# Preparing the later layers' weights in nine steps among a convolution's groups

## The chip, the cores and the metric

The kernel runs on one core of one Trainium2 chip. The metric is the device time of one execution in microseconds (us). Before the change the median of three timed runs is 3836.9 us; the three lie between 3829.45 and 3837.47 us. One further execution was profiled: it took 3831.74 us, and its span on the profile (first instruction to last) is 3829.9 us, so 1.84 us lie around the span.

## The reference, cut to what matters

Four layers follow one another on `x` of shape (4, 96, 64, 64), float32. Layer 0 is a pair of scan blocks with a fused normalisation; layer 1 is a depthwise 7x7 convolution and a two-layer perceptron; layer 2 is attention without softmax and a quantised perceptron; layer 3 is a Fourier mixer and another quantised perceptron. The change touches layer 1's convolution and the parameters of everything after it:

```python
# layer 1: the convolution, then the perceptron
h = jax.lax.conv_general_dilated(x, conv_w, window_strides=(1, 1), padding=((3, 3), (3, 3)),
        dimension_numbers=('NCHW', 'OIHW', 'NCHW'), feature_group_count=dim)
h = h + conv_b[None, :, None, None]
h = jnp.transpose(h, (0, 2, 3, 1))
h = (h - mu) * jax.lax.rsqrt(var + LN_EPS) * ln_g + ln_b
h = jax.nn.gelu(jnp.einsum('bhwc,cf->bhwf', h, w1) + b1, approximate=False)
h = jnp.einsum('bhwf,fc->bhwc', h, w2) + b2
h = jnp.transpose(h, (0, 3, 1, 2)) * layer_scale[None]
return h + x
# layer 3's mixer: a normalisation with given mean and variance on each side of it
def _bn(v, gamma, beta, mean, var):
    return (v - mean) * (gamma / jnp.sqrt(var + EPS)) + beta
h = jnp.einsum('bnc,hc->bnh', x, w1)
h = jax.nn.relu(_bn(h, bn1_gamma, bn1_beta, bn1_mean, bn1_var))
...
o = jnp.einsum('bnh,ch->bnc', y, w2)
return _bn(o, bn2_gamma, bn2_beta, bn2_mean, bn2_var)
```

The kernel folds these scales and shifts into the weights once: `ln_g` into `w1`, `ln_b` into `b1`, `layer_scale` into `w2` and `b2`, `bn1` into layer 3's `w1` (with a 97th row for the shift), `bn2` into its `w2`; and it rounds the weights of the two quantised perceptrons to an 8-bit type.

## The kernel before, in words

The program runs layer 0, then layer 1, layer 2, the Fourier mixer and the last perceptron, each with its own tile pools. Layer 1 (`layer1`, L909) has two parts. The first holds a manual schedule for TensorE (PE), VectorE (DVE), ScalarE (ACT) and GpSimd (POOL): on those four engines the instructions stand in the order in which the Python code issues them. The queue of SyncE (SP), which issues every DMA, is not in that list; a scheduler orders it, and it may put a DMA ahead of the place where the code asks for it.

The first part of layer 1 loads layer 0's output in 16 chunks and turns it so that a partition is a pixel position of a pair of image rows (L948 to L953). Then comes the convolution, a loop of 24 groups of four channels (L973). For each group, SP loads a banded matrix `band` of 128 x 2048 float32, 1024 KB (L957), into one of three buffers. PE makes 16 products of 128 x 128 from it (L983 three times and L986 once for each channel), and the result is evicted with the bias from PSUM by ACT for even groups (L993) and by DVE for odd ones (L991), four instructions each. POOL copies `x2` for the products of L986 two groups at a time (L964, L965). The PSUM tile of a group has four buffers (`cv`); a band's buffer is free again when its group's products are done, so the band of group g + 3 can be asked for when group g ends.

Ahead of group 8 stands one call, `consts2` (L975 calls L821), which prepares all later layers' weights. On PE it issues three products for `c_b1` (L836) and two for `a_w2` (L899). On ACT it issues two square roots (L878 for the first norm, L120 for the second). On DVE it issues everything else, in this order: the layer 1 weights (L839 to L846), the two perceptrons' roundings (L860 to L870, once for "f2" and once for "f3"), the first norm (L879 to L884), the second norm (L121 to L890), the scaled identity `bn2_d` (L895) and the copies of `a_w2` out of PSUM (L900). It asks for 17 loads. Three matter below: `wkv` and `a_w1` have 97 partitions, and so has `bn1_rows` (L876), where a row of 4 x 192 numbers is read 97 times, once for each partition:

```python
rows = wk.tile([C + 1, 4, NF], F32, name="bn1_rows")
nc.sync.dma_start(rows, ins["bn1_rows"].partition_broadcast(C + 1))
```

The raw weights of "f2" and "f3" share one buffer for each kind (tags `raww1` and `raww2`), so the second load waits until the first has been rounded.

Of the kernel before, what the change touches and what calls it, by code (L numbers as in the profile page):

```python
# [9 lines left out]
F32 = mybir.dt.float32  # L10
# [3 lines left out]
AF = mybir.ActivationFunctionType  # L14
# [4 lines left out]
B, C, HW, L = 4, 96, 64, 4096  # L19
# [6 lines left out]
HID = 384  # L26
N1, N2, NF = 128, 32, 192
# [75 lines left out]
class Net:  # L103
# [715 lines left out]


    def consts2(self, wk, small):  # L821
        tc, nc, ins = self.tc, self.nc, self.ins
        pool = self.pool2

        def load(name, shape, dtype=F32):
            t = pool.tile(shape, dtype, name=name)
            nc.sync.dma_start(t, ins[name])
            return t


        self.c_w1 = load("c_w1", [C, HID])
        self.c_w2 = load("c_w2", [128, 3, C])
        self.c_b1 = pool.tile([128, 3], F32, name="c_b1s")
        ps = small(128, 4)
        for m in range(3):
            nc.tensor.matmul(  # L836
                ps[:, m : m + 1], self.c_w1[:, m * 128 : (m + 1) * 128], self.v("c_ln_b"), start=True, stop=True
            )
        nc.vector.tensor_add(self.c_b1, self.v128("c_b1", 0, 3), ps[:, :3])  # L839
        nc.vector.tensor_scalar_mul(self.c_w1, self.c_w1, self.v("c_ln_g"))  # L840
        ls = wk.tile([128, C], F32, name="ls_row")
        nc.sync.dma_start(ls, ins["ls_row"].partition_broadcast(128))
        for m in range(3):
            nc.vector.tensor_mul(self.c_w2[:, m, :], self.c_w2[:, m, :], ls)
        self.c_b2 = pool.tile([C, 1], F32, name="c_b2s")
        nc.vector.tensor_mul(self.c_b2, self.v("c_b2"), self.v("c_ls"))  # L846


        self.wkv = load("wkv", [C + 1, 2 * C])
        self.wqt = load("wqt", [C, C + 1])  # L850
        self.wff = load("wff", [C, C])
        self.mask = load("mask", [C, C])


        self.ffn = {}
        for k in ("f2", "f3"):
            a = wk.tile([C, HID], F32, name="w1raw", tag="raww1")
            nc.sync.dma_start(a, ins[f"{k}_w1"])
            w1 = pool.tile([C, HID], F8, name=f"{k}w1q")
            nc.vector.tensor_copy(w1, a, saturate=False)  # L860
            a = wk.tile([128, 3, C], F32, name="w2raw", tag="raww2")
            nc.sync.dma_start(a, ins[f"{k}_w2"])
            w2 = pool.tile([128, 3, C], F8, name=f"{k}w2q")
            nc.vector.tensor_copy(w2, a, saturate=False)
            b1 = pool.tile([128, 3], F32, name=f"{k}b1q")
            b2 = pool.tile([C, 1], F32, name=f"{k}b2q")
            for b, src in ((b1, self.v128(f"{k}_b1", 0, 3)), (b2, self.v(f"{k}_b2"))):
                q = wk.tile(list(b.shape), F8, name="bq", tag=f"bq{b.shape[0]}{k}")
                nc.vector.tensor_copy(q, src, saturate=False)
                nc.vector.tensor_copy(b, q)  # L870
            self.ffn[k] = (w1, w2, b1, b2)


        self.a_w1 = load("a_w1", [C + 1, NF])
        rows = wk.tile([C + 1, 4, NF], F32, name="bn1_rows")
        nc.sync.dma_start(rows, ins["bn1_rows"].partition_broadcast(C + 1))  # L876
        s1 = wk.tile([C + 1, NF], F32, name="bn1_s")
        nc.scalar.activation(s1, rows[:, 3, :], AF.Sqrt, bias=self.eps[: C + 1])  # L878
        nc.vector.reciprocal(s1, s1)  # L879
        nc.vector.tensor_mul(s1, s1, rows[:, 0, :])  # L880
        nc.vector.tensor_mul(self.a_w1[:C], self.a_w1[:C], s1[:C])
        shift = wk.tile([C + 1, NF], F32, name="bn1_b")
        nc.vector.tensor_mul(shift, s1, rows[:, 2, :])
        nc.vector.tensor_sub(self.a_w1[C:], rows[C:, 1, :], shift[C:])  # L884
        r = self.rsqrt(pool, self.v("v2"), "bn2_r")
        self.s2 = pool.tile([C, 1], F32, name="bn2_s")
        nc.vector.tensor_mul(self.s2, r, self.v("g2"))
        self.b2 = pool.tile([C, 1], F32, name="bn2_b")
        nc.vector.tensor_mul(self.b2, self.s2, self.v("m2"))
        nc.vector.tensor_sub(self.b2, self.v("be2"), self.b2)  # L890

        raw = wk.tile([C, NF], F32, name="a_w2raw")
        nc.sync.dma_start(raw, ins["a_w2"])
        gain = wk.tile([C, C], F32, name="bn2_d")
        nc.vector.tensor_scalar_mul(gain, self.ident[:C, :C], self.s2)  # L895
        self.a_w2 = pool.tile([C, 2, C], F32, name="a_w2s")
        for half in range(2):
            ps = small(C, C)
            nc.tensor.matmul(ps, raw[:, half * C : (half + 1) * C], gain, start=True, stop=True)  # L899
            nc.vector.tensor_copy(self.a_w2[:, half], ps)  # L900
        self.dft1 = load("dft1", [N1, 2 * 65])
        self.twid = load("twid", [128, 2, 2 * 65])
        self.dft2 = load("dft2", [128, 3 * 128])
        self.dft64 = load("dft64", [128, 2, 128])

    def layer1(self, scratch, t):  # L909
        tc, nc, ins = self.tc, self.nc, self.ins  # L910
# [3 lines left out]
        with ExitStack() as ctx:  # L914
# [4 lines left out]
            with (  # L919
# [35 lines left out]
                def load(g):  # L955
                    w = wk.tile([128, GC, 4, 128], F32, name="band", tag="band", bufs=3)
                    nc.sync.dma_start(w, ins["band"][g])  # L957
                    return w

                def outer(g):  # L960

                    x2 = wk.tile([128, 2 * GC, B, NR], F32, name="x2", tag="x2", bufs=3)
                    at = slice(g * 2 * GC, (g + 1) * 2 * GC)
                    nc.gpsimd.tensor_copy(x2[:64], xt[:64, at, :, 4:])  # L964
                    nc.gpsimd.tensor_copy(x2[64:], xt[64:, at, :, :NR])  # L965
                    return x2

                def small(rows, cols):
                    ps = psum.tile([128, 4, 128], F32, name="w_ps", tag="xt", bufs=4)
                    return ps.rearrange("p a c -> p (a c)")[:rows, :cols]  # L970

                x2 = [outer(0)]
                for g in range(C // GC):  # L973
                    if g == 8:
                        self.consts2(wk, small)  # L975
                    if g % 2 == 0 and g + 2 < C // GC:
                        x2.append(outer(g // 2 + 1))
                    w = load(g)
                    ps = psum.tile([128, GC, B, NR], F32, name="cv_ps", tag="cv", bufs=4)
                    for d in range(GC):  # L980
                        c = g * GC + d
                        for k, j in enumerate((1, 0, 2)):
                            nc.tensor.matmul(  # L983
                                ps[:, d], w[:, d, j], xt[:, c, :, 1 + j : 1 + j + NR], start=k == 0, stop=False
                            )
                        nc.tensor.matmul(ps[:, d], w[:, d, 3], x2[g // 2][:, g % 2 * GC + d], start=False, stop=True)  # L986
                    for d in range(GC):
                        c = g * GC + d
                        dst = xt[:, c, :, 2 : 2 + NR]
                        if g % 2:  # L990
                            nc.vector.tensor_scalar_add(dst, ps[:, d], cb[:, c : c + 1])  # L991
                        else:
                            nc.scalar.activation(dst, ps[:, d], AF.Identity, bias=cb[:, c : c + 1])  # L993

            wk = ctx.enter_context(tc.tile_pool(name="l1w", bufs=1))
            psum = ctx.enter_context(tc.tile_pool(name="l1p", bufs=1, space=PSUM))
            mv, rs, xc, g = {}, {}, {}, {}
# [684 lines left out]
```

## Time and profile before

| what | before |
|---|---|
| median of three timed runs | 3836.9 us |
| their range | 3829.45 to 3837.47 us |
| the profiled execution's own time | 3831.74 us |
| its span | 3829.9 us |
| busy share of the span: PE, DVE, ACT, POOL | 84%, 78%, 71%, 67% |
| first product of the convolution (PE, L983) | at 2593.17 us |
| first eviction of group 0 (ACT, L993) | at 2601.18 us |
| first eviction of group 23 (DVE, L991) | at 2710.17 us |

All times on the trace count from the start of the span. A row of the timeline gives start, duration, engine, line, operation, output and inputs, sizes, a count, and in brackets how long the engine sat idle before it and what ended that. A matrix product in float32 appears as two instructions on PE, so the 16 products of a group are 32 rows in count. "SPq" rows are the DMA issues of SyncE: their duration is that of the issue, not of the transfer.

### The profile page before, as it was taken

Reading aid. Unit: us, or ns where it says so; the run is one execution under the profiler, and the core shown is the slowest. Engines: PE = TensorE matmul, PEld = TensorE weight load, DVE = VectorE, ACT = ScalarE, POOL = GpSimd, SP = SyncE. Lnnn points to the kernel's source line nnn. Section 1 sums busy time; section 2 is a strip of 40 time slices with the busy share of each in tenths; the row PEclk is TensorE's granted clock in tenths of the full one; section 3 lists DMA queues with packets and bytes.
Section 4 is the critical chain, followed back from the end, with each engine's and each line's share of the span. In section 5 each row is a group of like instructions: output and inputs, shape, how many; then the busy total and the mean of one; then the engine's idle time right before and its main releaser. Section 6 shows DMA issues by size and latency. Waiting matters only on the chain. (4 is left out here: it accounts for less than half of the span.)

```text
span 3829.9 us, 46555 instructions
## 1 busy us (share of the span) xinstructions
PE 3229.4 (84%) x15326; PEld 1475.1 (39%) x15326; DVE 2988.8 (78%) x2644; ACT 2719.1 (71%) x5456; POOL 2569.1 (67%) x922
## 2 busy tenths in 40 slices
PE   7888788888888888888888888657799998999988
PEld 3333233333323332333333333226544534766643
DVE  5999999999999999999999999962573384444649
ACT  6788888877887888788877787641355686666557
POOL 1988888888988888888888888832001064444427
PEclk8899998989998899889988898757899999999999
DMA  7566665666566656665665566556200000011101
GB/s 189 145 157 155 169 157 142 167 153 158 139 165 158 154 142 165 158 152 144 160 163 149 147 160 159 132 143 209 71 1 0 1 1 6 18 37 33 39 9 58
DMA packets 171642, 446.61 MB, mean 117 GB/s; under 512 B 48756, under 2 KB 50750, under 8 KB 168064
## 3 DMA queue, kind: packets, MB, share of 16 engines
q1 hardware_dynamic: 171400, 443.64, 45.2%
q8 instruction: 121, 1.98, 0.2%
q14 instruction: 121, 0.99, 0.1%
HBM read 369.97 MB, written 73.50 MB: 116 GB/s over the span
## 5 line engine op out<-in xcount | busy, mean ns | idle before, releaser
L648 POOL TENSOR_TENSOR hs<-hs,crep 128x2048 f32<-128x2048 f32 x384 | 1599.1, 4184 | 212.8 <-DVE hs L643 115.6
L610 ACT ACTIVATE da<-ddb,nega 128x1024 f32<-128x1024 f32 x576 | 657.8, 1147 | 192.3 <-DVE hs L643 187.4
L643 DVE TENSOR_TENSOR_SCAN hs<-da,state,rep 128x1024 f32<-128x1024 f32 x288 | 667.5, 2337 | 56.6 <-PE rep L594 40.5
L665 PE MATMUL y<-hs,sel_r 128*32 128x512 f32 x3072 | 455.4, 677 | 77.9 <-POOL hs L648 77.9
L621 POOL TENSOR_TENSOR up<-udb,brep 128x1024 f32<-128x1024 f32 x192 | 452.3, 2363 | 70.1 <-DMA udb<-ud 60.4
L594 PE MATMUL rep<-ident,uta 128*128 128x128 f32 x1536 | 242.3, 309 | 163.3 <-DVE hs L643 163.2
L507 ACT ACTIVATE uta<-delta,bt 128x192 f32<-128x192 f32 x1024 | 379.1, 442 | 1.1
L643 DVE TENSOR_TENSOR_SCAN hs<-dap,state,up 128x1024 f32<-128x1024 f32 x144 | 336.7, 2338 | 44.8 <-ACT dap L610 44.8
L643 DVE TENSOR_TENSOR_SCAN hs<-da,state,u 128x1024 f32<-128x1024 f32 x144 | 338.1, 2348 | 15.5 <-DVE u L636 0.5
L287 PE MATMUL ps<-n,w_x 97*64 97x512 f32 x1536 | 347.4, 600 | 1.5 <-ACT n L401 1.5
L594 PEld LDWEIGHTS rep<-ident,uta 128*128 128x128 f32 x1536 | 195.7, 158 | 268.5 <-DVE hs L643 148.8
L610 ACT ACTIVATE dap<-ddb,nega 128x1024 f32<-128x1024 f32 x192 | 213.9, 1114 | 101.3 <-DVE hs L643 100.7
L599 PE MATMUL rep<-dbl,sel_b 32*128 32x512 f32 x768 | 247.4, 723 | 27.8 <-DVE hs L643 27.0
L636 DVE TENSOR_TENSOR u<-udb,rep 128x1024 f32<-128x1024 f32 x192 | 235.7, 1227 | 39.6 <-DMA udb<-ud 13.7
L1240 POOL CAST hq<-y 128x1536 fp8e5<-128x1536 f16 x64 | 94.0, 1469 | 217.8 <-issue 122.6
L287 PE MATMUL ps<-dbl,dtw 103*64 103x512 f32 x384 | 174.4, 960 | 74.5 <-ACT dbl L441 74.5
L636 DVE TENSOR_TENSOR rep<-udb,rep 128x1024 f32<-128x1024 f32 x192 | 231.9, 1208 | 0.0
L643 DVE TENSOR_TENSOR_SCAN hs<-da,rep 128x1024 f32<-128x1024 f32 x96 | 216.8, 2277 | 15.8 <-PE rep L594 10.6
L665 PEld LDWEIGHTS y<-hs,sel_r 128*32 128x32 f32 x3072 | 68.2, 116 | 383.0 <-POOL hs L648 194.8
L287 PEld LDWEIGHTS ps<-n,w_x 97*64 97x64 f32 x1536 | 110.1, 137 | 232.8 <-issue 206.2
L479 POOL TENSOR_TENSOR delta<-delta,xc 128x1536 f32<-128x1536 f32 x31 | 106.6, 3438 | 94.4 <-DMA dd<-delta 87.7
L1379 POOL TENSOR_TENSOR av<-av,ec 128x780 f32<-128x780 f32 x32 | 58.8, 1838 | 133.2 <-ACT av L1376 133.2
(276 smaller groups left out, 6228.6 us busy)
## 6 DMA issues: line engine op xcount, KB each, us to landing
ddb<-dd SPq DMA_DIRECT2D x768, 128.0 KB
udb<-ud SPq DMA_DIRECT2D x768, 128.0 KB
crep<-cd SPq DMA_DIRECT2D x512, 128.0 KB
dd<-delta SPq DMA_DIRECT2D x64, 384.0 KB
band<-in_band SPq DMA_DIRECT2D x24, 1024.0 KB
ud<-delta SPq DMA_DIRECT2D x62, 384.0 KB
brep<-cd SPq DMA_DIRECT2D x128, 128.0 KB
x<-in_x SPq DMA_DIRECT2D x32, 384.0 KB
```

The source lines that it names most:

```text
L287: nc.tensor.matmul(ps[rows], w[:, 64 * p : 64 * p + 64], rhs[:, at.start + shift : at.stop + shift], start=k == 0, stop=k == len(ws) - 1, ...
L479: (nc.gpsimd if k else nc.vector).tensor_mul(m["du"], m["delta"], m["xc"])
L507: nc.scalar.mul(m["uta"][:, q, :, 32 * s4 : 32 * s4 + 32].rearrange("t (p j) d -> t p j d", p=3), m["udt"][:, :, q].rearrange("t p (j d) - ...
L594: nc.tensor.transpose(x[:, q * 128 : q * 128 + 128], made[k]["uta"][:, q, 2 * h + j], self.ident)
L599: nc.tensor.matmul(x[:, at], sel_b[rows, g], made[k]["dbl"][rows, at], start=True, stop=True)
L610: nc.scalar.activation(da, made[k]["dd", h, j], AF.Exp, scale=nega[:, col : col + 1])
L621: nc.gpsimd.tensor_mul(up, made[k]["ud", p][:, j], made[k]["brep", GP])
L636: nc.vector.tensor_mul(u, made[k]["ud", h][:, j], x)
L643: nc.vector.tensor_tensor_scan(hs[:, 1:], made[k].pop(("da", t)), u, st, ALU.mult, ALU.add)
L648: nc.gpsimd.tensor_mul(hs[:, :, :T], hs[:, :, 1:], twice(made[k]["crep", g]))
L665: nc.tensor.matmul(made[k]["y", p][row : row + 32], sel_r, made[k]["hs", p, g][:, j, at], start=False, stop=True, skip_group_check=True,)
L1240: nc.gpsimd.tensor_copy(q, y2, saturate=False)
```

## The change

`consts2` becomes a generator. Its body is cut into nine steps by `yield`; the loop over the groups runs one step ahead of each of the groups 4, 5, 6, 7, 14, 15, 16, 17 and 20, instead of all of it ahead of group 8. The first four steps only ask for loads; the raw weights of "f2" and "f3" get buffers of their own. The next five compute. The four vectors of the first norm are loaded as one row on one partition, the arithmetic on them is done on that one partition, and a product with a column of ones spreads scale and shift over 97 partitions. The rest of the arithmetic is the same.

```diff
-        def load(name, shape, dtype=F32):
-            t = pool.tile(shape, dtype, name=name)
+        def load(name, shape, dtype=F32, into=pool, key=None):
+            t = into.tile(shape, dtype, name=key or name)
             nc.sync.dma_start(t, ins[name])
             return t
         self.c_w1 = load("c_w1", [C, HID])
         self.c_w2 = load("c_w2", [128, 3, C])
+        ls = wk.tile([128, C], F32, name="ls_row")
+        nc.sync.dma_start(ls, ins["ls_row"].partition_broadcast(128))
+        self.wkv = load("wkv", [C + 1, 2 * C])
+        self.wqt = load("wqt", [C, C + 1])
+        yield
+        self.wff = load("wff", [C, C])
+        self.mask = load("mask", [C, C])
+        raw = {k: load(f"{k}_w1", [C, HID], into=wk, key=f"{k}w1raw") for k in ("f2", "f3")}
+        raw |= {k + "2": load(f"{k}_w2", [128, 3, C], into=wk, key=f"{k}w2raw") for k in ("f2", "f3")}
+        yield
+        self.a_w1 = load("a_w1", [C + 1, NF])
+        rows = wk.tile([1, 4, NF], F32, name="bn1_rows")
+        nc.sync.dma_start(rows, ins["bn1_rows"])
+        araw = load("a_w2", [C, NF], into=wk, key="a_w2raw")
+        self.dft1 = load("dft1", [N1, 2 * 65])
+        yield
+        self.twid = load("twid", [128, 2, 2 * 65])
+        self.dft2 = load("dft2", [128, 3 * 128])
+        self.dft64 = load("dft64", [128, 2, 128])
+        yield
...
+        yield
         self.ffn = {}
         for k in ("f2", "f3"):
-            a = wk.tile([C, HID], F32, name="w1raw", tag="raww1")
-            nc.sync.dma_start(a, ins[f"{k}_w1"])
             w1 = pool.tile([C, HID], F8, name=f"{k}w1q")
-            nc.vector.tensor_copy(w1, a, saturate=False)
-            a = wk.tile([128, 3, C], F32, name="w2raw", tag="raww2")
-            nc.sync.dma_start(a, ins[f"{k}_w2"])
+            nc.vector.tensor_copy(w1, raw[k], saturate=False)
             w2 = pool.tile([128, 3, C], F8, name=f"{k}w2q")
-            nc.vector.tensor_copy(w2, a, saturate=False)
+            nc.vector.tensor_copy(w2, raw[k + "2"], saturate=False)
...
             self.ffn[k] = (w1, w2, b1, b2)
-        self.a_w1 = load("a_w1", [C + 1, NF])
-        rows = wk.tile([C + 1, 4, NF], F32, name="bn1_rows")
-        nc.sync.dma_start(rows, ins["bn1_rows"].partition_broadcast(C + 1))
-        s1 = wk.tile([C + 1, NF], F32, name="bn1_s")
-        nc.scalar.activation(s1, rows[:, 3, :], AF.Sqrt, bias=self.eps[: C + 1])
-        nc.vector.reciprocal(s1, s1)
-        nc.vector.tensor_mul(s1, s1, rows[:, 0, :])
-        nc.vector.tensor_mul(self.a_w1[:C], self.a_w1[:C], s1[:C])
-        shift = wk.tile([C + 1, NF], F32, name="bn1_b")
-        nc.vector.tensor_mul(shift, s1, rows[:, 2, :])
-        nc.vector.tensor_sub(self.a_w1[C:], rows[C:, 1, :], shift[C:])
+            yield
+        s1 = wk.tile([1, 2, NF], F32, name="bn1_s")
+        one = wk.tile([1, C + 1], F32, name="bn1_one")
+        nc.vector.memset(one, 1.0)
+        nc.scalar.activation(s1[:, 0], rows[:, 3, :], AF.Sqrt, bias=self.eps[:1])
+        nc.vector.reciprocal(s1[:, 0], s1[:, 0])
+        nc.vector.tensor_mul(s1[:, 0], s1[:, 0], rows[:, 0, :])
+        nc.vector.tensor_mul(s1[:, 1], s1[:, 0], rows[:, 2, :])
+        nc.vector.tensor_sub(s1[:, 1], rows[:, 1, :], s1[:, 1])
...
+        yield
+        ps = small(C + 1, 2 * NF)
+        nc.tensor.matmul(ps, one, s1.rearrange("p k f -> p (k f)"), start=True, stop=True)
+        nc.vector.tensor_mul(self.a_w1[:C], self.a_w1[:C], ps[:C, :NF])
+        nc.vector.tensor_copy(self.a_w1[C:], ps[C:, NF:])
...
+                later = self.consts2(wk, small)
                 x2 = [outer(0)]
                 for g in range(C // GC):
-                    if g == 8:
-                        self.consts2(wk, small)
+                    if g in (4, 5, 6, 7, 14, 15, 16, 17, 20):
+                        next(later)
```

More of the change, by code (lines that the diff above doesn't have):

```diff
@@ L840, in consts2 @@
         nc.vector.tensor_scalar_mul(self.c_w1, self.c_w1, self.v("c_ln_g"))
-        ls = wk.tile([128, C], F32, name="ls_row")
-        nc.sync.dma_start(ls, ins["ls_row"].partition_broadcast(128))
         for m in range(3):
@@ L846, in consts2 @@
         nc.vector.tensor_mul(self.c_b2, self.v("c_b2"), self.v("c_ls"))
[L849 to L852, printed above, removed]
+        yield
         self.ffn = {}
         for k in ("f2", "f3"):
-            a = wk.tile([C, HID], F32, name="w1raw", tag="raww1")
-            nc.sync.dma_start(a, ins[f"{k}_w1"])
             w1 = pool.tile([C, HID], F8, name=f"{k}w1q")
-            nc.vector.tensor_copy(w1, a, saturate=False)
-            a = wk.tile([128, 3, C], F32, name="w2raw", tag="raww2")
-            nc.sync.dma_start(a, ins[f"{k}_w2"])
+            nc.vector.tensor_copy(w1, raw[k], saturate=False)
             w2 = pool.tile([128, 3, C], F8, name=f"{k}w2q")
-            nc.vector.tensor_copy(w2, a, saturate=False)
+            nc.vector.tensor_copy(w2, raw[k + "2"], saturate=False)
             b1 = pool.tile([128, 3], F32, name=f"{k}b1q")
@@ L890, in consts2 @@
         nc.vector.tensor_sub(self.b2, self.v("be2"), self.b2)
-        raw = wk.tile([C, NF], F32, name="a_w2raw")
-        nc.sync.dma_start(raw, ins["a_w2"])
         gain = wk.tile([C, C], F32, name="bn2_d")
         nc.vector.tensor_scalar_mul(gain, self.ident[:C, :C], self.s2)
+        yield
[3 more added lines that the diff above has]
+        nc.vector.tensor_copy(self.a_w1[C:], ps[C:, NF:])
         self.a_w2 = pool.tile([C, 2, C], F32, name="a_w2s")
@@ L898, in consts2 @@
             ps = small(C, C)
-            nc.tensor.matmul(ps, raw[:, half * C : (half + 1) * C], gain, start=True, stop=True)
+            nc.tensor.matmul(ps, araw[:, half * C : (half + 1) * C], gain, start=True, stop=True)
             nc.vector.tensor_copy(self.a_w2[:, half], ps)
[L901 to L904, printed above, removed]
+        yield
     def layer1(self, scratch, t):
```

## The prediction

> **What bounds the kernel now.** The layers run one after the other, so I looked for the stage that the change touches. The page's 40 slices show a dip in PE's busy share (6, 5) and clock (8, 7, 5, 7) around slice 27; the page's chain of waits covers only 14% of the span and does not reach back to it. I then cut layer 1 with the view by windows (window, length, busy us of PE and PEld, DVE, ACT, POOL, granted PE clock, DMA share, GB/s):
>
> ```profile
> 2590.00:2626.00 36.00, 33.25 (x259) 32.53 (x260) 5.55 (x15) 5.38 (x17) 12.45 (x12) 0.85 0.62 213
> 2626.00:2650.00 24.00, 1.72 (x16) 1.67 (x15) 8.38 (x32) 0.64 (x2) 2.07 (x2) 0.61 0.51 167
> 2650.00:2713.00 63.00, 60.05 (x516) 59.86 (x514) 11.00 (x42) 9.16 (x32) 10.38 (x10) 0.96 0.63 218
> ```
>
> PE is full before and after, and works 1.72 us of the 24 between. The convolution is bound by PE, with one hole in it. The timelines of PE, ACT and DVE show what holds it open:
>
> ```profile
> 2622.98 0.91 PE L983 MATMUL cv_ps<-xt,band 128*128 128x128 f32 x6 [0.51 <-DMA band<-in_band]
> ...
> 2626.63 0.73 PE L836 MATMUL w_ps<-vec,c_w 96*128 96x1 f32 x6
> 2649.63 0.93 PE L899 MATMUL w_ps<-bn_d,a_w2raw 96*96 96x96 f32 x4 [22.28 <-DVE bn_d L895]
> ...
> 2622.57 1.14 ACT L993 ACTIVATE xt<-cv_ps,cb 128x128 f32<-128x128 f32 x4 [6.01 <-PE cv_ps L986]
> 2637.37 0.46 ACT L878 ACTIVATE bn_s<-bn_rows,eps 97x192 f32<-97x192 f32 x1 [13.66 <-DMA bn_rows<-in_bn_rows]
> ...
> 2656.51 1.15 ACT L993 ACTIVATE xt<-cv_ps,cb 128x128 f32<-128x128 f32 x4 [18.50 <-PE cv_ps L986]
> ...
> 2626.90 1.13 DVE L991 TENSOR_SCALAR xt<-cv_ps,cb 128x128 f32<-128x128 f32 x4 [6.77 <-PE cv_ps L986]
> ...
> 2644.69 0.35 DVE L860 CAST f3w1q<-w1raw 96x384 fp8e5<-96x384 f32 x1 [13.86 <-DMA w1raw<-in_f_w]
> ```
>
> PE's two `a_w2` products (L899) stand ahead of group 8 and wait 22.28 us for `bn_d`. That is last in DVE's queue, which waits 13.86 us for the raw "f3" weights. SP's own rows say why they are late:
>
> ```profile
> 2615.72 0.30 SPq L876 DMA_DIRECT2D bn_rows<-in_bn_rows  x1
> 2616.06 6.70 SPq L893 DMA_DIRECT2D a_w2raw<-in_a_w  x1
> ...
> 2637.41 0.33 SPq L858 DMA_DIRECT2D w1raw<-in_f_w  x1
> ```
>
> The "f3" load is issued only at 2637.41, when `bn1_rows` has landed, 21.6 us after its issue.
>
> **What the Trainium skill says.** (1) "DMA: Bandwidth & Descriptors", section "Why a DMA increments its semaphore by 16 and not by 1": a load is split over k engines, k the largest number up to 16 that divides the slowest dimension; 96 or 128 partitions give 16. By that rule 97, a prime, gives 1: `bn1_rows`, `a_w1` and `wkv` each go through one engine. The trace agrees in effect: 291 KB took 21.6 us, and the DMA share fell to 0.19 between 2620 and 2625. (2) "TensorE: Matmul & The Clock Gate", Part 1: PE idle for some 3.4 us drops to half clock and needs as long again to return. The trace agrees: after the hole the clock is 0.50 until 2655, and a conv product's instruction takes up to 552 ns there against 273. (3) "Perfetto Trace Analysis", "Per-instruction lifecycle": a DMA's reported duration leaves out the data's movement. Here 0.30 us of issue stand for a 21.6 us load, so I take landing times from who waited.
>
> **The change, part by part.**
>
> *The hole.* Evictions give the cadence: ACT's at 2608.26, 2615.41 and 2622.57 (timeline) are two groups apart, so a group takes 3.58 us. From DVE's for group 7 (2626.90) to ACT's for group 8 (2656.51) it is 29.61: 26.03 too long. That contains 22.28 of waiting, 0.73 for L836, some 0.7 for L899 and about 2.3 of half clock. All goes from this place: **-26.03**.
>
> *The band's wait.* From 2622.57 to 2626.90 is 4.33: group 7 lost 0.75 to its band. It is counted anew below: **-0.75**.
>
> *PE's work that stays.* The three `c_b1` products (0.73) move ahead of group 14, the two `a_w2` products ahead of group 20. At full clock a 128-column product costs 3.58/16 = 0.22 us, so two of 96 columns cost some 0.4 with their start. New is the spreading product, 384 columns: 3 x 0.22 = 0.67. Together **+1.8**.
>
> *DVE, ACT and their waits.* In the order of the built kernel, steps 14 and 15 both stand between DVE's evictions of groups 13 and 15, and steps 16 and 17 between those of 15 and 17. From the DVE rows: 2.1 us for step 14, 1.3 each for 15 and 16, 3.4 for 17. The one-partition form doesn't shorten it: the subtraction on one partition took 0.35 us for 192 columns, like the products on 97. So 3.4 and 4.7 us go into gaps of 6.03: hidden. New wait: DVE's reciprocal waits for ACT's square root, behind ACT's eviction of group 16. If E is the end of group 16 on PE, the root is ready at E + 1.14 + 0.46, the chain of 3.4 ends near E + 5.0, and queued behind it is DVE's eviction of group 17, due at E + 3.6: 1.4 us late. PSUM has four buffers, so PE needs that one at about E + 14: nothing. PE's wait ahead of group 20 is due at E + 10.7, 5.7 us after `bn_d`: nothing. Without that cover each us there would cost one. ACT's two roots (0.74) lie in its 6.01 of idle. POOL's queue is unchanged.
>
> *The loads.* There are 17 as before; SP issues each in 0.3 to 0.4 us, which PE does not see. `bn1_rows` shrinks from 298 kB on one engine to 3 kB. But the other 97-row load, `a_w1` (74.5 kB), now stands before band 6 instead of before band 7, and 590 kB of raw weights stand before band 5. A band is asked for when a buffer frees and is needed 2 x 3.58 = 7.15 us later. I follow the one busy engine, taking it to work in order. Its rate: `bn1_rows` came 14.4 us after band 7 (2622.95 to 2637.37), so 298/14.4 = 20.7 kB/us for short rows. By the "f3" weights' arrival, 7.3 us later, it had moved its sixteenths of two bands and five small loads, 178 kB: 24.3 kB/us. A band's sixteenth (65.5 kB) costs 2.7 us, `a_w1` 3.6. Before: band 6 asked at 2611.8, done 2614.5, `a_w1` 2618.1, band 7 2620.8; PE began at 2622.98, so 2.2 us lie around. After: band 4 asked at 2604.6, done 2607.3; raw weights 1.8, to 2609.1; band 5 to 2611.8; `a_w1` to 2615.4; three small loads to 2616.0; band 6 to 2618.7, usable 2620.9, needed 2618.9: **+2.0**. Then 1.4 for the Fourier tables, band 7 to 2622.8, usable 2625.0, needed 2624.5 (already shifted): **+0.5**. Band 8 is in time. Bounds: 0 if an engine moves the 27 GiB/s that page (1) gives under "Specifications" (an estimate: `a_w1` then takes 2.6 and a band 2.3, and band 6 is usable near 2617.9, in time); 10 if SP is held at two places as at `a_w2raw` (6.70 us), less the cover of some 2 each. Below nothing is excluded: waiting for data cannot gain.
>
> *Sum:* -26.03 - 0.75 + 1.8 + 2.5 = **-22.5**. Against the profiled run, 3831.7 - 22.5 = 3809.2. The median of the timed runs, 3836.9, lies 5.2 above it; the four times known (3829.5, 3831.7, 3836.9, 3837.5) have their middle at 3834.3, and I take that as the base: 3834.3 - 22.5 = **3811.8** is the forecast. What is late next is PE itself: groups at 3.58 to the end; the perceptron follows unchanged.
>
> **The rivals.**
>
> *A, as above,* 3804 to 3818. For it: bands came at PE's pace from 2656 to 2700 with SP waiting on PE each time.
>
> *B, the loads take the hole's place.* Too much before bands 5 to 8 makes PE wait about 2 us at five groups, or 10 at one with a fall of the clock (2.3). Saving 12: 3822. For it: SP was held 6.70 us once, and 5.97 at `wqt` behind `wkv`'s 97 rows. Against: DMA moved 294 to 339 GB/s between 2605 and 2615 without delaying a product.
>
> *C, the steps don't hide.* The chain is late by more than its 5.7 us and PE waits at group 20 as it did from 2644.69 (4.9, and 2.3 of clock). Saving 15: 3819. Against: the gaps above.
>
> *D, slower.* With PE unbroken from 2593 to 2920 its granted clock falls in layer 1's perceptron. PE is busy 224 of the 247 us from 2713. A clock of 0.91 there costs 22 us, the whole gain; 0.87 costs 33, so 3845. It decides from 0.91 down. Against: from 2760 to 3180 the clock is 1.00 with PE nearly full.
>
> **How the numbers follow.** A 0.80, B 0.13, C 0.04, D 0.03. 0.2% is 7.7 us, about what a measurement of this kernel tells from no change. A and C are faster; I give 0.03 of B to "same": faster 0.94, same 0.03, slower 0.03. Range: from the lowest run with no band wait (3829.5 - 25.0 = 3804.5, rounded down to 3803) to B (3822, rounded up to 3823).
>
> **What would show it.** Right: PE's groups 3.58 apart from group 1 to 23 except at groups 6, 7, 14 and 20; the first eviction of group 23 some 86.5 us after that of group 0, instead of 108.99; clock 1.00 from 2605 to the stage's end; no product waiting for `bn_d`. Wrong: waits for `band` of over 5 us, SP rows of several us near `a_w1`, PE idle before L902 or L908, or a lower clock after the convolution.

## The result and the profile after

The changed kernel takes 3807.45 us (median of four runs, 3803.28 to 3811.07), the kernel before 3834.56 us beside it (four runs, 3829.45 to 3837.47). The ratio is 0.9933, 95% interval 0.9921 to 0.9946: a gain of 27.1 us, by the interval 20.7 to 30.3. The profiled execution took 3803.84 us, its span is 3801.7 us.

First the stage that the prediction was about: the view by windows, cut as before at PE's start, at the old hole's place and at the stage's end.

```profile
2583.00:2619.00 36.00, 31.21 (x244) 30.43 (x245) 5.85 (x15) 5.38 (x17) 12.46 (x12) 0.87 0.77 262
2619.00:2643.00 24.00, 23.76 (x213) 23.60 (x213) 3.38 (x12) 3.43 (x12) 6.23 (x6) 1.00 0.81 288
2643.00:2682.00 39.00, 38.15 (x336) 37.27 (x334) 16.57 (x55) 6.22 (x22) 6.41 (x6) 1.00 0.65 227
```

Where PE worked 1.72 of 24 us it now works 23.76, at full clock. DVE's preparation is in the third window (16.57 us busy), beside PE's 38.15 of 39. PE's own timeline shows the waits for bands that are left, and the moved products (two more waits of 0.1 us, at groups 5 and 7, are too short to be marked):

```profile
2613.94 0.91 PE L987 MATMUL cv_ps<-xt,band 128*128 128x128 f32 x6 [2.24 <-DMA band<-in_band]
2632.41 0.91 PE L987 MATMUL cv_ps<-xt,band 128*128 128x128 f32 x6 [0.24 <-DMA band<-in_band]
2643.21 0.73 PE L857 MATMUL w_ps<-vec,c_w 96*128 96x1 f32 x6
2665.43 0.88 PE L902 MATMUL w_ps<-bn_s,bn_one 1*97 1x384 f32 x2
2666.24 0.58 PE L908 MATMUL w_ps<-bn_d,a_w2raw 96*96 96x96 f32 x4
```

No bracket stands behind L902 or L908: PE did not wait for the norms. It waited at group 6 (2.24 us) and a little at group 11 (0.24) for a band. SP's rows around that place:

```profile
2600.90 0.33 SPq L960 DMA_DIRECT2D band<-in_band  x1
2601.27 0.29 SPq L828 DMA_DIRECT2D a_w<-in_a_w  x1
2601.61 2.98 SPq L845 DMA_DIRECT2D bn_rows<-in_bn_rows  x1
...
2605.52 0.37 SPq L960 DMA_DIRECT2D band<-in_band  x1
```

SP is held for 2.98 us at the tiny `bn_rows`, right behind the 97-partition `a_w1` (`a_w` in the rows), and so asks for band 6 about 1 us late: at 2605.52, 0.97 us after the eviction of group 3 began, where bands 3 to 5 were asked for shortly before such an eviction began. PE gets it at 2613.94. SP's own waits tell when `a_w1` landed:

```profile
SPq L960 <- DMA a_w<-in_a_w: 2.7, 1, 2.7
```

The request for band 7 waits 2.7 us for that landing and goes out at 2610.89; 3.05 us later PE has band 6.

The measure used below is the **stage**: from the first eviction of group 0 to the first of group 23. It was 108.99 us (2601.18 to 2710.17) and is 87.37 (2593.89 to 2681.26): 21.62 less. The spans differ by 28.2. The rest lies elsewhere: the stage starts 7.29 earlier, and what follows it takes 0.71 longer (1120.44 against 1119.73).

### The profile page after: what moved, and what is told of

Its sections match the earlier page's. It is cut to its first block, busy times and chain, and to the rows that moved or that the text cites. A ratio compares the mean times of both kernels' runs of the same rounds, so it can differ in the third digit from the quotient of the medians.

```text
span 3801.7 us, 46563 instructions
## 1 busy us (share of the span) xinstructions
PE 3222.8 (85%) x15328; PEld 1469.6 (39%) x15328; DVE 2992.1 (79%) x2646; ACT 2720.4 (72%) x5456; POOL 2569.4 (68%) x922
```

## The experiments

Each kernel is one edit of the kernel before or of the changed one. Stages are read from each one's profiled execution, one for each row. Ratios are to the kernel before on the same chip: its median was 3832.23 us beside the split rows, the one row, the old rows and the split `a_w1`, and 3832.61 beside the four others that are not the two kernels above.

| kernel | stage, us | gained | median, us | ratio, 95% interval |
|---|---|---|---|---|
| before | 108.99 | | | |
| changed | 87.37 | 21.6 | 3807.45 | 0.9933 (0.9921 to 0.9946) |
| before, rows split 96 + 1 | 98.17 | 10.8 | 3816.33 | 0.9964 (0.9950 to 0.9977) |
| before, one row | 99.27 | 9.7 | 3823.57 | 0.9975 (0.9967 to 0.9983) |
| before, own raw buffers | 100.39 | 8.6 | 3826.14 | 0.9984 (0.9977 to 0.9991) |
| changed, old rows | 100.85 | 8.1 | 3824.99 | 0.9983 (0.9976 to 0.9991) |
| changed, computing at group 8 | 98.00 | 11.0 | 3824.72 | 0.9979 (0.9971 to 0.9986) |
| changed, `a_w1` split | 85.79 | 23.2 | 3810.46 | 0.9953 (0.9938 to 0.9968) |
| changed, loads spread evenly | 84.28 | 24.7 | 3808.64 | 0.9940 (0.9926 to 0.9953) |
| changed, once more | 88.22 | 20.8 | 3812.29 | 0.9947 (0.9934 to 0.9960) |

In every row the gain of the stage lies within the interval of the median. The medians alone stray from the stages by up to 5 us (the split rows gain 15.9 by the median, computing at group 8 gains 7.9), so what follows rests on the stages and on the waits within them.

**The rows in two DMAs.** Is it the bytes of `bn1_rows`, or that 97 partitions go through one DMA engine? The bytes stay:

```diff
-        nc.sync.dma_start(rows, ins["bn1_rows"].partition_broadcast(C + 1))
+        nc.sync.dma_start(rows[:C], ins["bn1_rows"].partition_broadcast(C))
+        nc.sync.dma_start(rows[C:], ins["bn1_rows"])
```

> The kernel before, with one edit: bn1_rows is read for 96 partitions in one DMA and for the 97th in a second; same bytes, same place, same arithmetic. Measured on the convolution's stage, from the first eviction of group 0 to the first of group 23 (before 108.99 us, after 87.37). Theory (the hole is held open because a 97-partition load runs through one DMA engine): the rows land within some 4 us, the raw f3 weights are asked for as soon as f2 is rounded (near 2630) and come some 4 us later, PE goes on near 2638 instead of 2649.6: stage 97 to 99 us, some 11 us less in time. Rival (the bytes of the broadcast, or the work in one place whatever the loads): stage stays within 3 us of 109.

Measured: 98.17, within the range of the theory. Of ACT's, DVE's and PE's timelines, the rows that answer to those shown of before:

```profile
2620.69 0.45 ACT L879 ACTIVATE bn_s<-bn_rows,eps 97x192 f32<-97x192 f32 x1 [1.24 <-DMA bn_rows<-in_bn_rows]
...
2629.32 0.36 DVE L860 CAST f3w1q<-w1raw 96x384 fp8e5<-96x384 f32 x1 [1.62 <-DMA w1raw<-in_f_w]
...
2634.22 0.93 PE L900 MATMUL w_ps<-bn_d,a_w2raw 96*96 96x96 f32 x4 [9.99 <-issue]
```

ACT has the rows 9.22 us after their issue at 2611.47, not the 4 us expected, but far from the 21.65 of before. DVE waits 1.62 us for the "f3" weights where it waited 13.86, and PE sits idle 9.99 us where it sat 22.28. The same 291 KB in 96 + 1 partitions shorten the hole by 12.3 us: bytes, place and arithmetic are as before, so it was the 97 partitions in one load (that such a load keeps a single engine busy is shown further down, with the old rows). SP's own waits in the kernel before show how the rows had held up the "f3" load:

```profile
SPq L858 <- DMA bn_rows<-in_bn_rows: 7.3, 1, 7.3
```

The "f2" weights had been rounded by 2630.3, and SP waited on for the rows to land. Of the 12.3 us, 7.3 are this wait; the other 5 are the "f3" load itself, in use 7.28 us after its issue before and 2.33 us here. A part of it comes back: PE now waits 1.63 us for band 7 (0.51 before), though the rows are asked for 0.4 us after that band.

**One row, work still in one place.**

> The kernel before with the changed kernel's one-row form of the first norm (one row, arithmetic on one partition, spreading product), all still ahead of group 8 and the raw weights still sharing buffers. Theory: as with the split rows, stage 97 to 100 us, the product adding 0.7 and some waits; so the row alone is worth about half of the gain of 21.6, and the spreading of the work the other half. Rival (the place of the work is all): stage near 109. Second rival (the row is all): stage near 88.

The edit is the changed kernel's one-row norm put into the old `consts2`. Measured: 99.27, within the range of the theory and far from both rivals. From PE's timeline:

```profile
2639.01 1.56 PE L886 MATMUL w_ps<-bn_s,bn_one 1*97 1x384 f32 x2 [8.79 <-DVE bn_s L884]
2642.38 0.93 PE L903 MATMUL w_ps<-bn_d,a_w2raw 96*96 96x96 f32 x4 [1.81 <-issue]
```

The row removes the late load; what is left, 8.79 and 1.81 us, is DVE's chain, for which PE's products stand and wait. (In the 8.79 are 1.53 us in which DVE waits for the "f3" weights, whose buffers are still shared.) The spreading product is at half clock there, 1.56 us against 0.88 in the changed kernel.

**The steps without the row.**

> The changed kernel with its nine steps, but the first norm in the old form (97-partition broadcast load in the third step, arithmetic on 97 partitions, no spreading product). Theory: the 298 kB on one engine now stand ahead of band 6 and PE waits there for 16 us instead of 2.2, with a fall of the clock: stage 101 to 105 us, so the steps without the row are worth only a third of the gain. Rival (the steps alone do it): stage 86 to 89 us.

The edit puts the 97-partition broadcast and the old arithmetic back into steps three and eight. Measured: 100.85, just under the range of the theory. First PE's timeline, then the view by windows over the wait:

```profile
2630.63 1.62 PE L983 MATMUL cv_ps<-xt,band 128*128 128x128 f32 x6 [15.05 <-DMA band<-in_band]
```

```profile
2610.00:2615.00 5.00, 5.00 (x47) 5.00 (x47) 0.00 (x0) 1.14 (x4) 0.68 (x1) 1.00 0.16 54
2615.00:2620.00 5.00, 0.58 (x6) 0.39 (x4) 1.12 (x4) 0.00 (x0) 2.07 (x2) 0.82 0.75 252
2620.00:2625.00 5.00, 0.00 (x0) 0.00 (x0) 0.00 (x0) 0.00 (x0) 0.00 (x0) 0.50 0.75 251
```

The hole has only moved, from `bn_d` to a band: 15.05 us at group 6. Ahead of it the DMA share is 0.16 at 54 GB/s. SP is held for 5.84 us at `a_w2raw`, behind the broadcast, and asks for band 6 only at 2614.88, so little new comes in. What is under way meanwhile goes through one engine of the sixteen, as a window of one microsecond shows:

```profile
2611.00:2612.00 1.00, 1.00 (x11) 1.00 (x11) 0.00 (x0) 0.00 (x0) 0.00 (x0) 1.00 0.07 23
```

A share of 0.07 is close to one sixteenth, 0.0625. The late request is not what keeps PE waiting: by SP's waits the broadcast lands at 2627.66 (the request for band 8 waits 6.0 us for it), and PE has band 6 2.97 us after that. From the landing of `a_w1` to band 6 it is 3.05 us in the changed kernel, 3.04 with the computing at group 8, 2.97 in the changed kernel's second execution. Band 6 comes last on the engine of the odd load. Spreading the work over the groups does not spread a load that sits on one engine.

**`a_w1` in two DMAs.** What keeps band 6 waiting in the changed kernel?

```diff
-        self.a_w1 = load("a_w1", [C + 1, NF])
+        self.a_w1 = pool.tile([C + 1, NF], F32, name="a_w1")
+        nc.sync.dma_start(self.a_w1[:C], ins["a_w1"][:C])
+        nc.sync.dma_start(self.a_w1[C:], ins["a_w1"][C:])
```

> The changed kernel with a_w1 loaded as 96 partitions and a 97th in two DMAs. Theory (band 6 is late because a_w1 keeps one DMA engine for 3.6 us): the wait of 2.24 us at group 6 goes, stage 84.5 to 85.5 us. Rival (the sixteen engines together are full with 590 kB of raw weights and the bands, the DMA share is 1.0 there): the wait stays near 2, stage 87.

Measured: 85.79, between the two. The wait at group 6 is gone, but two others appear. PE's timeline, then the windows ahead of them:

```profile
2621.27 0.91 PE L989 MATMUL cv_ps<-xt,band 128*128 128x128 f32 x6 [0.16 <-DMA band<-in_band]
2629.62 0.91 PE L989 MATMUL cv_ps<-xt,band 128*128 128x128 f32 x6 [0.95 <-DMA band<-in_band]
```

```profile
2616.00:2621.00 5.00, 5.00 (x46) 4.92 (x45) 1.12 (x4) 0.00 (x0) 2.07 (x2) 1.00 1.05 356
2621.00:2626.00 5.00, 4.84 (x44) 4.76 (x43) 0.80 (x4) 1.14 (x4) 0.78 (x1) 1.00 1.02 386
```

With the load spread all sixteen engines are full (share 1.05 and 1.02, 356 and 386 GB/s; in the changed kernel it is as high there, 1.08 from 2602 to 2605), and a band still comes 0.95 us late; SP, which waits 2.3 us for band 5 to land ahead of a Fourier table, had also asked for it about 1 us late, at 2622.06. So both explanations hold for a part. Beside the kernel in which no band is late (84.28, below) the stage has 1.5 us here, 3.1 in the changed kernel and 3.9 in its second execution: the one engine is half of the lateness or more, the crowding of the loads the rest.

**Computing in one place, loads early.**

```diff
-                    if g in (4, 5, 6, 7, 14, 15, 16, 17, 20):
+                    for _ in range({4: 1, 5: 1, 6: 1, 7: 1, 8: 5}.get(g, 0)):
                         next(later)
```

> The changed kernel with its four loading steps as they are, but its five computing steps all ahead of group 8. Theory (two causes: late loads, and a chain of DVE work that PE must sit out where its own products stand right behind it): the loads are early here, so what is left is DVE's chain, 1.1 for the eviction of group 7 and 8.1 of preparation, less 0.7 of PE's own products, then half a clock (2.3): stage 97 to 100 us, near the split rows. Rival (once the loads are early the place of the computing is free): stage 86 to 89.

Measured: 98.00, within the range of the theory. From PE's timeline:

```profile
2644.24 1.56 PE L902 MATMUL w_ps<-bn_s,bn_one 1*97 1x384 f32 x2 [7.08 <-DVE bn_r L121]
```

With every parameter in time (DVE waits for none) PE still idles 7.08 us ahead of group 8, and then runs at half clock. From group 7's eviction to group 8's it is 16.21 us instead of 3.56. Late bands cost 3.2 us at groups 5 to 7, as in the changed kernel, so what differs is the placing of the computing: it is worth 10.6 of the 21.6.

**Own buffers for the raw weights.**

```diff
-            a = wk.tile([C, HID], F32, name="w1raw", tag="raww1")
+            a = wk.tile([C, HID], F32, name="w1raw", tag=f"raww1{k}")
```

and the same for `w2raw`.

> The kernel before, with one edit: the raw weights of f2 and f3 have buffers of their own, so the f3 loads need not wait for f2's rounding; bn1_rows stays a 97-partition broadcast. Theory: the f3 weights are early, but the broadcast lands near 2638.7 on the scale of the trace before, and DVE's chain for the norms (3.7 us) starts only then: PE goes on near 2643 instead of 2649.6, stage 100 to 104 us, so own buffers alone are worth a quarter to a third of the gain. Rival (the shared buffers were the cause): stage 92 to 96.

Measured: 100.39, within the range of the theory. From ACT's timeline:

```profile
2635.24 0.45 ACT L878 ACTIVATE bn_s<-bn_rows,eps 97x192 f32<-97x192 f32 x1 [14.00 <-DMA bn_rows<-in_bn_rows]
```

The "f3" weights are no longer waited for, and the next one in the row, the broadcast itself, holds ACT for 14.00 us and through it DVE and PE (15.42 us idle). One thing came free: the scheduler moved `a_w1` behind band 7 here, and PE's wait for band 7 (0.51) vanished. That is a second sign of what `a_w1` costs a band behind it.

**Loads spread evenly.** The steps of loading become ten, ahead of the groups 4 to 13, with a few small loads each, and `a_w1` is split; the computing stays. Of the edit, the loop:

```diff
-                    if g in (4, 5, 6, 7, 14, 15, 16, 17, 20):
+                    if g in (4, 5, 6, 7, 8, 9, 10, 11, 12, 13, 14, 15, 16, 17, 20):
```

> The changed kernel with its loads spread over the groups 4 to 13, one or two small ones ahead of each band and at most 180 KB, and a_w1 in 96 partitions and one; computing as it is. Theory: no band is late any more; the stage is 23 x 3.58 and PE's own 2.0, 84.0 to 84.8 us, 3 us less than the changed kernel, which the time itself (runs lie 8 us apart) can hardly show. Rival (bands are late for another reason, the sixteen engines being near their limit all the time): waits of 1 us or more stay somewhere, stage over 85.5.

Measured: 84.28, within the range of the theory. The view of PE's waits from the first product to the stage's end has one row:

```profile
PE cv_ps L1000 <- POOL x L978: 0.6, 1, 0.6
```

It is the wait of the first group for POOL. No band is late, and PE's own added work, 1.94 us, is all that is above 23 groups of 3.58. The median is 3808.64 beside 3812.29 for the changed kernel in the same session: that points the way of the stage's 3.9, but runs of each of these two kernels lie up to 11 us apart and the intervals overlap, so the time alone doesn't show it.

**The changed kernel once more.**

> The changed kernel again, unchanged. Its profiled run gained 28.1 us against the profiled run of before, of which the stage gave 21.6 and the time ahead of it 7.3. Theory (what lies ahead of the stage differs by some us from run to run, whatever the kernel): stage 86.5 to 88.5 again, but the first eviction of group 0 anywhere between 2590 and 2607, and a median gain of 21 to 25 over many runs. Rival (the change also shortens what lies ahead): the first eviction again 6 us or more ahead of 2601, and a median gain of 27 or more.

Measured: stage 88.22, first eviction of group 0 at 2596.31, median gain 20.3 (15.3 to 25.3 by its interval), from five runs; that is just under the range of the theory. Over all ten profiled executions, kernels of before and of after mixed, that first eviction lies between 2593.89 and 2608.58, and both kernels at that place issue the same instructions. The mean is 2600.2 over the four that come from the kernel before and 2600.3 over the six that come from the changed one. So the 7.3 us ahead of the stage are not the change's: the run shown happened to be early.

## Why the prediction was right

**The mechanism** was right. The hole is gone: from group 7's eviction to group 8's it is 3.56 us (predicted 3.58, before 29.61). The experiments show its two causes, which the prediction had read from one chain: the late load through one engine (split rows, 10.8 us of stage) and DVE's chain behind which PE's products stood (computing at group 8). Neither half alone gives more than 11.0; together they give 21.6.

**The terms of the sum**, on the stage:

| term | predicted | measured |
|---|---|---|
| the hole | -26.03 | -26.05 |
| band 7's old wait | -0.75 | -0.75, counted anew in the bands below |
| PE's moved and added products | +1.8 | +0.65 at group 14, +1.33 at group 20 |
| late bands | +2.0 at group 6, +0.5 at group 7 | +2.46 at group 6, +0.23 at groups 5 and 7 together, +0.48 at group 11 |
| sum | -22.5 | -21.6 |

The place and size of the late band were right, and at group 6 so was the reason. Following the one engine in order, the prediction had band 6 in use 16.3 us after band 4 was asked for (2604.6 to 2620.9); it was 16.62 (2597.32 to 2613.94). It left out that the sixteen engines together are full there: with `a_w1` split, 1.5 us of lateness stay. It also priced every issue at 0.3 to 0.4 us, and SP was held for 2.98 us behind `a_w1`: a sign of being wrong that it had named itself. PE lost nothing to it that shows, since band 6, though asked for late, had to follow `a_w1` on the one engine. Group 11's 0.48 it did not foresee; in the second execution group 11 has no wait, and group 18 has one of 0.39, so the small waits change place from run to run. That there are 17 loads is a miscount, they are 18; nothing rests on it.

**DVE** was mis-sized without effect. Its eviction of group 17 was to be 1.4 us late and was 2.7: the interval from group 16's is 6.25 instead of 3.58. Three instructions took 1.15, 1.23 and 0.81 us where 0.30, 0.35 and 0.15 were counted (last section). The four PSUM buffers covered it, as said: PE waited for nothing at L902 and L908.

**The base.** The forecast 3811.8 was 3834.3 - 22.5; the median of before was 3834.56 and that of after 3807.45. The missing 4.4 us are not in the stage. They lie within what the runs differ by ahead of it, since the second measurement of the same kernel gained 20.3. The forecast gain of 22.5 lies between the two.

**The rivals.** B's mechanism was real but small (3.2 us of late bands, not 10); with the old rows it appears in full, 15.05 us at one place. C did not occur. D is refuted: the granted clock after the convolution is as before (1.00 from 2731 to 3151, where the kernel before had 1.00 from 2760 to 3180), and the rest of the program took 0.7 us longer, not 22.

## What to carry to other kernels

A load's partition count can matter more than its bytes: 97 partitions (96 channels and a bias row) kept one DMA engine of sixteen busy for some 12 to 14 us (an estimate from 298 kB at 25 to 20.7 kB/us), for part of it with the others idle, and what was queued behind it on that engine came late; the same load as 96 + 1, or one row spread by a product, does not. Work that one engine does between the products of another should be placed several steps ahead of the product that needs it, not right before it. And a load moved off one path lands on another: ask which transfer stands behind it, and give each group no more than its DMA engines have left.

## What the runs showed that was not expected

**DVE and POOL.** Some DVE instructions that meet a POOL copy last until about that copy's end. From the timelines of DVE and of POOL in the changed kernel:

```profile
2658.49 1.23 DVE L890 TENSOR_TENSOR bn_s<-bn_rows,bn_s 1x192 f32<-1x192 f32 x1
```

```profile
2658.48 1.04 POOL L967 COPY x<-xt 64x1024 f32<-64x1024 f32 x1 [4.88 <-PE cv_ps L990]
```

The subtraction on one partition ends 0.2 us after the copy of 1.04 us that started with it. With the computing at group 8 no copy runs then, and the same line took 0.35 us. L893 (0.81 against 0.15) and L873 (1.15 against 0.30) fit in the same way. But not every meeting costs DVE time. With `a_w1` split the same subtraction (L892 there) met a copy too:

```profile
2670.00 0.35 DVE L892 TENSOR_TENSOR bn_s<-bn_rows,bn_s 1x192 f32<-1x192 f32 x1
```

```profile
2670.00 1.25 POOL L969 COPY x<-xt 64x1024 f32<-64x1024 f32 x1 [4.89 <-PE cv_ps L992]
```

Here the copy is the longer one, 1.25 us instead of 1.04: it looks as if one of the two waits for the other. The Trainium skill, "GPSIMD Engine Reference", section "Key points", says that GpSimd shares its SBUF interfaces with VectorE and contends with VectorE instructions that have two SBUF inputs or run in a 2-port mode. L890 and L893 have two such inputs, and the reciprocal between them (L121), with one, kept its 0.14 us beside a copy, so the trace agrees; in what mode L873 ran, with its one input, no trace shows. All this is read from coincidences in the timelines, and no run here moved the copies to test it.

**What SP waits for.** In every kernel here but the one with the loads spread evenly, SP has to wait somewhere in the stage for an earlier load to land before it issues the next DMA, and each such wait named in this text is for the DMA eight places before. In the kernel before, the "f3" load is the eighth after `bn_rows`; in the changed kernel band 7 is the eighth after `a_w1`. So a slow load holds up not only what shares its engine but also the eighth DMA behind it and all that stands behind that. The prediction had seen that the "f3" load goes out when the rows land, without saying why. What in the program or the chip sets the eight, no run shows.

Left open: why band 7 is later with the rows split (1.63 against 0.51 us), though the rows are asked for after it. By SP's waits `a_w1`, which stands ahead of band 7, landed there at 2616.86, 8.97 us after its issue, and band 7 followed 2.99 us later as elsewhere; when `a_w1` landed in the kernel before, no view tells. The order of issue alone does not tell when a load lands.
